# Two-layer graph network on one core: block turns behind the statistics, narrower edge-count columns, PSUM banks handed over singly

## Chip, cores and metric

One core of a Trainium2 chip. The metric is device microseconds of one execution, the median of several. PE is TensorE's matmul pipe, PEld its weight loads, DVE is VectorE, ACT ScalarE, POOL GpSimd, SP SyncE.

## Reference, cut to what matters

`N = 4096` nodes, 512 features, `adj` 4096 x 4096. Layer 0 is attention inside graphs of 128 nodes, layer 1 is graph attention over `adj`:

```python
h = relu(layernorm(x));  x = x + graph_attention(h, adj, ptr, Wq, Wk, Wv, ...)   # layer 0
h = relu(layernorm(x))
mx = einsum('nf,hfd->hnd', h, W)                                                 # layer 1, 8 heads of 64
attn = softmax(where(adj > 0, s_i + t_j, -inf))
x = x + einsum('hij,hjd->hid', attn, mx)
```

The factor from `s_i` cancels in the softmax, so the kernel forms e^t * mx and e^t for each node (520 numbers), multiplies them by the 0/1 mask, and divides.

## The kernel before

Layer 1 has two stages that matter here. Between the layers (about 360 to 460 us of the trace), each of 32 row tiles is normalised, transposed and projected (`project1`), then weighed by e^t on DVE (`weigh`) and split into a high and a low part. Tiles below 16 ("near") are transposed on PE. Tiles from 16 ("far") are turned on DVE in blocks of 32, written to DRAM and read back in the right layout. The far work runs eight tiles ahead of the projection. The order of DVE, ACT, POOL and SP is that of the source:

```python
for i in range(n, NT):
    far, near = i + AHEAD, i + 2
    if near + 1 < MIXED: load(near + 1)
    load(far + 2)
    if MIXED < far <= NT: turn(far - 1)              # DVE, waits for ACT's relu of that row
    if far % BY == 1 and MIXED + BY < far <= NT + 1: move(far // BY - 1)
    ...                                              # cut: first mask tile
    low()                                            # POOL: low part of tile i - 2
    if far < NT:     of[far] = moments(rows[far])    # DVE statistics, POOL rstd
    if near < MIXED: of[near] = moments(rows[near])
    if i + 1 < MIXED: relu_T(ps_t, rows[i + 1], hTs[i + 1])      # PE transposes, ACT relu
    pm = project1(ps_p, hTs[i], w1x)                 # PE, 8 matmuls
    if before: low = finish(*before, later=True)     # DVE weighing, ACT cast
    if near < MIXED: norm(rows[near], rows[near], of[near])
    if far < NT:     norm(rows[far], rows[far], of[far])
    e = weights(i, pm)                               # ACT exponential
    ...                                              # near tiles: four products on ACT
    if far < NT: nc.scalar.activation(rows[far], rows[far], AF.Relu)
```

Then the aggregation (about 460 to 950 us): for each row tile, 32 inner tiles times three column groups of 2 x 174 columns (high and low part of 174 numbers), accumulated in PSUM:

```python
D, H, EC, CB, CW1 = 512, 8, 520, 3, 174             # 3 * 174 = 522: two columns of ones count edges
def product(pg, at, part, j, c):
    nc.tensor.matmul(
        pg[:, : 2 * CW1], at[:, j, :], part(j)[:, c].rearrange("p s w -> p (s w)"),
        start=(j == 0), stop=(j == NT - 1),
    )
ps_g = straight.enter_context(tc.tile_pool(name="ps_g3", bufs=2, space=PSUM))
```

The edge count itself is used only in a general branch that these inputs do not take.

Of the kernel before, what the change touches and what calls it, by code (L numbers as in the profile page):

```python
# [23 lines left out]
NT = N // P  # L24
# [29 lines left out]
def kernel(  # L54
# [248 lines left out]
        widen(at, turn_words(sb, load_words(sb, i)))  # L303
        return at

    def product(pg, at, part, j, c):

        nc.tensor.matmul(  # L308
            pg[:, : 2 * CW1], at[:, j, :], part(j)[:, c].rearrange("p s w -> p (s w)"),
            start=(j == 0), stop=(j == NT - 1),  # L310
        )

    def aggregate(sb, ps_g, at, part):

        pg = ps_g.tile([P, CB, 512], F32, name="pg")
        for j in range(NT):
            for c in range(CB):
                product(pg[:, c], at, part, j, c)
        tot = sb.tile([P, EW], F32, name="tot")
        tot3 = tot.rearrange("p (c w) -> p c w", c=CB)  # L320
        nc.scalar.copy(tot3, pg[:, :, :CW1])  # L321
        nc.vector.tensor_tensor(tot3, tot3, pg[:, :, CW1 : 2 * CW1], ALU.add)  # L322
        return tot
# [48 lines left out]
    with ExitStack() as straight:  # L372
# [4 lines left out]
        with ExitStack() as prep:  # L377
# [262 lines left out]
            with tc.manual_schedule(engines={E.DVE, E.Activation, E.Pool, E.SP}):  # L640
                n = len(ahead) - 1
                hTs[n] = ahead[n]
                before = None
                for i in (1, 2):
                    load(n + i)
                for i in range(MIXED, n + AHEAD + 2):
                    load(i)
                norm(rows[n + 1], rows[n + 1])
                low = lambda: None
                for i in range(n, NT):  # L650
                    far, near = i + AHEAD, i + 2
                    if near + 1 < MIXED:
                        load(near + 1)
                    load(far + 2)
                    if MIXED < far <= NT:
                        turn(far - 1)
                    if far % BY == 1 and MIXED + BY < far <= NT + 1:
                        move(far // BY - 1)
                    if far == NT + 1:

                        begun.close()
                        sb3a = straight.enter_context(
                            tc.tile_pool(name="sb3a", bufs=1, side="right", reuse_waits="tile")
                        )
                        ata = sb3a.tile([P, NT, P], F32R, name="ata")
                        words = load_words(sb3a, 0)
                    if i == NT - 4:
                        at8 = turn_words(sb3a, words)
                    if i in (NT - 3, NT - 2):
                        half = (i - NT + 3) * NW // 2  # L670
                        widen(ata, at8, half, half + NW // 2)
                    low()
                    if far < NT:
                        of[far] = moments(rows[far])
                    if near < MIXED:
                        of[near] = moments(rows[near])
                    if i + 1 < MIXED:
                        hTs[i + 1] = sb2.tile([P, KC, P], F32, name="hT1")
                        relu_T(ps_t, rows[i + 1], hTs[i + 1])
                    pm = project1(ps_p, hTs[i], w1x)  # L680
                    if before:
                        low = finish(*before, later=True)
                    if near < MIXED:
                        norm(rows[near], rows[near], of[near])
                    if far < NT:
                        norm(rows[far], rows[far], of[far])
                    e = weights(i, pm)
                    halves = (1, 0)
                    if i < MIXED:
                        halves = (0,)  # L690
                        for h in range(H // 2, H):
                            nc.scalar.mul(
                                e[:, ts(h, HD)], pm[1][:, ts(h - H // 2, HD)],
                                e[:, ES + h : ES + h + 1],
                            )
                    before = (e, pm, part_tile(lo if i < LO else hi, i), halves)
                    if far < NT:
                        nc.scalar.activation(rows[far], rows[far], AF.Relu)  # L698
                low()
                finish(*before)  # L700
# [4 lines left out]
        sb3 = straight.enter_context(  # L705
            tc.tile_pool(name="sb3", bufs=2, side="right", reuse_waits="tile")
        )
        ps_g = straight.enter_context(tc.tile_pool(name="ps_g3", bufs=2, space=PSUM))
        nc.gpsimd.memset(held, 1.0)

        atb = sb3.tile([P, NT, P], F32R, name="atb", bufs=1)
# [46 lines left out]
        for c in (CB - 1, 0, 1):  # L758
            if c == 1:
                pg = ps_g.tile([P, CB, 512], F32, name="pg")[:, 0]  # L760
            else:
                pg = ps_l.tile([P, 512], F32, name="pl")
            for j in range(NT):
                product(pg, at, lambda j: parts[j], j, c)
            part = tot[:, ts(c, CW1)]
            nc.scalar.copy(part, pg[:, :CW1])
            nc.vector.tensor_tensor(part, part, pg[:, CW1 : 2 * CW1], ALU.add)
            if c == CB - 1:
                r = heads_rest(tot)
                nc.vector.tensor_scalar(held[:, 5:6], tot[:, ES : ES + 1], 0.0, None, ALU.is_gt)  # L770
                all_held = small.tile([P, 1], F32, name="all_held")
                nc.vector.tensor_reduce(all_held, held, AX.X, ALU.min)
                nc.vector.tensor_copy(
                    rb[:, :D].rearrange("p (h d) -> p h d", d=HD),
                    r[:, :, None].to_broadcast([P, H, HD]),
                )
            if c == 0:
                pt = ps_g.tile([P, CB, 512], F32, name="pg")[:, 0, :P]
                nc.tensor.transpose(pt[:1, :], all_held, ident)
                least = small.tile([1, 1], F32, name="least")  # L780
                nc.vector.tensor_reduce(least, pt[:1, :], AX.X, ALU.min)
                nc.vector.tensor_scalar(bad_i, least, 1.0, None, ALU.is_lt)
            here = slice(c * CW1, min((c + 1) * CW1, D))
            nc.vector.tensor_tensor(tot[:, here], tot[:, here], rb[:, here], ALU.mult)
            nc.vector.tensor_tensor(tot[:, here], tot[:, here], row[:, here], ALU.add)
            nc.scalar.dma_start(out[ts(i, P), here], tot[:, here])
# [3 lines left out]
    with tc.If(bad > 0, label="general"):  # L790
# [131 lines left out]
        with (  # L922
# [60 lines left out]
            with tc.For_i(0, n_levels, 1):  # L983
# [29 lines left out]
                with (  # L1013
                    tc.tile_pool(name="sb5", bufs=1) as sb,
                    tc.tile_pool(name="ps_g5", bufs=1, space=PSUM) as ps_g,
                    tc.For_i(0, NT, 1) as i,
                ):
                    sofar = sb.tile([P, D], F32, name="sofar")
                    nc.sync.dma_start(sofar, out[ds(i * P, P), :])
                    at = load_mask(sb, i, sb.tile([P, NT, P], F32R, name="at"))  # L1020
                    tot = aggregate(sb, ps_g, at, lambda j: parts_e[:, j])
                    alone = small.tile([P, 1], F32, name="alone")
                    nc.vector.tensor_scalar(alone, tot[:, EC : EC + 1], 0.0, None, ALU.is_equal)
                    n_alone = small.tile([P, 1], F32, name="n_alone")
                    nc.vector.tensor_scalar(n_alone, alone, float(N), None, ALU.mult)
                    den = small.tile([P, H], F32, name="den")
                    nc.vector.tensor_scalar(den, tot[:, ES:EC], n_alone, 1e-30, ALU.add, ALU.max)
                    num = tot[:, :D]
                    nc.vector.scalar_tensor_tensor(num, mx_sum, alone, num, ALU.mult, ALU.add)
                    row = done[:, ds(i, 1), :].rearrange("p o h -> p (o h)")  # L1030
                    take = small.tile([P, H], F32, name="take")
                    nc.vector.tensor_scalar(take, den, ACCEPT, None, ALU.is_ge)
                    nc.vector.tensor_tensor(take, take, row, ALU.is_gt)
                    nc.vector.tensor_add(row, row, take)
                    r = small.tile([P, H], F32, name="r")
                    nc.vector.reciprocal(r, den)
                    nc.vector.tensor_mul(r, r, take)
                    scaled(num, r)
                    nc.vector.tensor_add(num, num, sofar)
                    nc.sync.dma_start(out[ds(i * P, P), :], num)  # L1040
# [38 lines left out]
```

## Time and profile before

| | before |
|---|---|
| time, median | 959.8 us (first three runs), 959.05 us (five runs) |
| span in the trace | 956.0 us |
| PE busy | 934.7 us |
| last transposes of `row` to first aggregation matmul | 360.37 to 460.46 us, 100.09 us |
| first start to last end of the aggregation's matmuls | 460.46 to 950.37 us, 489.91 us |

The last two rows cut the trace at marks, so that drift of the first 360 us stays out. I call the first of them the passage. Its marks in PE's timeline of before (columns: start, length, engine, line, operation, tiles, shapes, count, and in brackets the idle time before and what ended it):

```profile
360.37 0.60 PE L136 MATMUL pt<-ident,row 128*128 128x128 f32 x4
460.46 15.53 PE L308 MATMUL pg<-part,ata 128*128 128x348 f32 x96 [0.61 <-DVE e L268]
```

Timeline of PEld in the kernel before:

```profile
408.52 3.37 PEld L259 LDWEIGHTS pp<-w1x,hT 128*128 128x128 f32 x16 [2.21 <-issue]
412.26 3.37 PEld L259 LDWEIGHTS pp<-w1x,hT 128*128 128x128 f32 x16 [0.37 <-issue]
415.96 3.37 PEld L259 LDWEIGHTS pp<-w1x,hT 128*128 128x128 f32 x16 [0.32 <-issue]
419.75 3.37 PEld L259 LDWEIGHTS pp<-w1x,hT 128*128 128x128 f32 x16 [0.41 <-issue]
```

The same time in the timeline of PE matmuls:

```profile
408.56 51.30 PE L259 MATMUL pp<-w1x,hT 128*128 128x264 f32 x224 [1.84 <-DVE e L268]
```

PE seems busy for 51.30 us without a break (this view joins records across idle times under 0.15 us; the busy time from 408.56 to the first aggregation matmul at 460.46 sums to 51.15 of 51.90 us). The loads show a break after every 16, that is after every tile, and tiles 3.74 us apart.

### The profile page before, as it was taken

Reading aid. Unit: us, or ns where it says so; the run is one execution under the profiler, and the core shown is the slowest. Engines: PE = TensorE matmul, PEld = TensorE weight load, DVE = VectorE, ACT = ScalarE, POOL = GpSimd, SP = SyncE. Lnnn points to the kernel's source line nnn. Section 1 sums busy time; section 2 is a strip of 40 time slices with the busy share of each in tenths; the row PEclk is TensorE's granted clock in tenths of the full one; section 3 lists DMA queues with packets and bytes.
Section 4 is the critical chain, followed back from the end, with each engine's and each line's share of the span. In section 5 each row is a group of like instructions: output and inputs, shape, how many; then the busy total and the mean of one; then the engine's idle time right before and its main releaser. Section 6 shows DMA issues by size and latency. Waiting matters only on the chain.

```text
span 956.0 us, 13142 instructions
## 1 busy us (share of the span) xinstructions
PE 934.7 (98%) x4987; PEld 810.8 (85%) x4987; DVE 465.0 (49%) x992; ACT 267.9 (28%) x539; POOL 179.9 (19%) x344
## 2 busy tenths in 40 slices
PE   8999999999999999999999999999999999999997
PEld 5676667776666777778999999999999999999997
DVE  4678877775775445674445242423324242423322
ACT  5776576666662224532000000000000000000000
POOL 2311213211211224655210100101010110101010
PEclk9999999999999999999999999999999999999999
DMA  9989889998985213575131312122231313222111
GB/s 343 417 344 390 332 312 364 348 367 322 367 349 199 78 34 110 165 198 133 56 85 49 88 50 84 51 82 72 61 89 45 89 50 83 57 77 85 48 45 36
DMA packets 61062, 156.63 MB, mean 164 GB/s; under 512 B 6722, under 2 KB 23490, under 8 KB 52290
## 3 DMA queue, kind: packets, MB, share of 16 engines
q1 hardware_dynamic: 51058, 138.70, 42.0%
q10 hardware_dynamic: 9936, 17.05, 4.8%
q8 instruction: 40, 0.66, 0.3%
q14 instruction: 28, 0.23, 0.1%
HBM read 117.97 MB, written 37.75 MB: 163 GB/s over the span
## 4 chain that ended last, share of the span: by engine, by line
PE 86%; DVE 4%; DMA 4%; ACT 3%; issue 1%; POOL 1%; SPq 0%; ACTq 0%; DVEq 0%
PE pg L308 50%; PE pp L457 12%; PE pp L445 10%; PE pp L259 5%; PE pp L530 3%; PE pss L503 3%; PE pt L136 1%; DMA row<-x_d 1%; DVE stats L118 1%; DMA a<-adj 1%; PE pl L308 1%; DVE blocks L623 1%; ACT rowm L698 1%; POOL rstd L124 1%; DMA mw<-a_d 1%
## 5 line engine op out<-in xcount | busy, mean ns | idle before, releaser
L308 PE MATMUL pg<-part,ata 128*128 128x348 f32 x1536 | 247.4, 322 | 0.6 <-DVE e L268 0.6
L308 PEld LDWEIGHTS pg<-part,ata 128*128 128x128 f32 x1536 | 245.0, 188 | 1.0 <-issue 1.0
L308 PE MATMUL pg<-part,atb 128*128 128x348 f32 x1472 | 237.3, 322 | 0.0
L308 PEld LDWEIGHTS pg<-part,atb 128*128 128x128 f32 x1472 | 235.0, 188 | 0.1
L321 ACT COPY tot<-pg 128x522 f32<-128x522 f32 x31 | 18.6, 599 | 455.9 <-PE pg L308 455.9
L480 ACT ACTIVATE junk<-a 128x2048 bf16<-128x2048 f32 (+15 forms) x92 | 124.5, 1353 | 49.9 <-DVE x L532 28.0
L259 PE MATMUL pp<-w1x,hT 128*128 128x256 f32 (+1 forms) x512 | 117.0, 384 | 2.0 <-DVE e L268 1.8
L457 PE MATMUL pp<-wv,hT 128*128 128x512 f32 x256 | 116.4, 598 | 0.0
L445 PE MATMUL pp<-hT,m_sb 128*128 128x256 f32 x512 | 113.2, 379 | 0.0
L259 PEld LDWEIGHTS pp<-w1x,hT 128*128 128x128 f32 x512 | 95.3, 190 | 19.3 <-issue 4.7
L296 DVE CAST atb<-at 128x4096 fp32r<-128x4096 fp8e4 x16 | 36.7, 2293 | 153.1 <-PE pg L308 153.1
L445 PEld LDWEIGHTS pp<-hT,m_sb 128*128 128x128 f32 x512 | 96.2, 190 | 12.8 <-issue 0.5
L296 DVE CAST ata<-at 128x4096 fp32r<-128x4096 fp8e4 (+1 forms) x17 | 37.3, 2196 | 141.8 <-PE pg L308 141.8
L457 PEld LDWEIGHTS pp<-wv,hT 128*128 128x128 f32 x256 | 49.2, 192 | 61.8 <-issue 61.8
L146 DVE TENSOR_SCALAR a<-a 128x512 fp8e4<-128x512 f32 x256 | 98.8, 466 | 1.6 <-DMA a_d<-a 1.4
L733 POOL COPY den_all<-tot 128x1 f32<-128x1 f32 x31 | 5.7, 184 | 367.9 <-DVE tot L322 355.9
L737 POOL TENSOR_TENSOR tot<-tot,row 128x512 f32<-128x512 f32 x31 | 39.9, 1286 | 61.9 <-DVE tot L327 57.8
L122 POOL TENSOR_SCALAR ve<-mv 128x1 f32<-128x1 f32 x64 | 16.3, 258 | 163.3 <-DVE mv L120 163.3
L243 POOL TENSOR_TENSOR part<-e,part 128x522 fp32r<-128x522 f32 x32 | 42.8, 1336 | 18.5 <-ACT part L240 18.4
L287 DVE STREAM_TRANSPOSE at<-mw 128x1024 f32<-128x1024 f32 x32 | 39.6, 1238 | 5.3 <-DMA mw<-a_d 5.3
L124 POOL TENSOR_TENSOR rstd<-ve,neghalf 128x1 f32<-128x1 f32 x64 | 38.5, 604 | 4.6
L461 DVE TENSOR_TENSOR v<-pp,bv_sb 128x512 f32<-128x512 f32 x32 | 22.0, 689 | 32.2 <-PE pp L457 32.2
(113 smaller groups left out, 691.0 us busy)
## 6 DMA issues: line engine op xcount, KB each, us to landing
a<-adj SPq DMA_DIRECT2D x64, 1024.0 KB, 12.8
a_d<-a SPq DMA_DIRECT2D x32, 512.0 KB, 10.1
mw<-a_d SPq DMA_DIRECT2D x128, 128.0 KB, 4.0
row<-x_d SPq DMA_DIRECT2D x41, 256.0 KB, 3.5
xg<-x SPq DMA_DIRECT2D x16, 512.0 KB, 4.6
x_d<-x ACTq DMA_DIRECT2D x32, 256.0 KB, 4.2
out<-tot ACTq DMA_DIRECT2D x31, 256.0 KB, 3.7
rowm<-x_d SPq DMA_DIRECT2D x16, 256.0 KB, 4.8
```

What stands on the lines that cost most here:

```text
L124: nc.gpsimd.tensor_tensor(rstd, ve, neghalf, ALU.pow)
L146: nc.vector.tensor_scalar(a8v[:, u], av[:, u], 0.0, None, ALU.is_gt, saturate=False)
L243: nc.gpsimd.tensor_sub(dst[:, :, 1, :], e3, dst[:, :, 0, :].bitcast(F32))
L259: nc.tensor.matmul(pm[g][:, :n], hT[:, k, :], w1x[:, k, g * HW : g * HW + n], start=(k == 0), stop=(k == KC - 1),)
L287: nc.vector.transpose(at8.rearrange("p c n b -> p (c n b)").bitcast(F32).rearrange("p (c u n) -> p c u n", c=NW, n=B), mw.rearrange("p u ( ...
L296: nc.vector.tensor_copy(at[:, c0 * BY : c1 * BY].rearrange("p (c b) q -> p c b q", b=BY), at8[:, c0:c1].rearrange("p c q b -> p c b q"),)
L308: nc.tensor.matmul(pg[:, : 2 * CW1], at[:, j, :], part(j)[:, c].rearrange("p s w -> p (s w)"), start=(j == 0), stop=(j == NT - 1),)
L445: nc.tensor.matmul(pp[:, : G * P], m_sb[:, k, ts(m, P)], hT[:, k, :], start=(k == 0), stop=(k == KC - 1),)
L457: nc.tensor.matmul(pp, hT[:, k, ts(t, P)], wv[:, k, :], start=(k == 0), stop=(k == KC - 1))
L480: nc.scalar.activation(junk[:, c0:c1], a[:, c0:c1], AF.Exp, scale=2.0 * NEG, accum_out=sums[:, n : n + 1],)
L503: nc.tensor.matmul(pss[:, t, :], gT[:, k, ts(t, P)], hT[:, k, ts(t, P)], start=(k == 0), stop=(k == KC - 1),)
L737: nc.gpsimd.tensor_add(num, num, row)
```

## The change

The intent: DVE need not wait for ACT's relu while statistics of another, loaded row could be taken; the columns of ones need no matmul except one that defines the PSUM cells; and the first aggregation tile needs only three banks, which were free long before.

```diff
-    def product(pg, at, part, j, c):
+    def product(pg, at, part, j, c, count):
+        n = CW1 if count or j == 0 else min(CW1, EC - c * CW1)
         nc.tensor.matmul(
-            pg[:, : 2 * CW1], at[:, j, :], part(j)[:, c].rearrange("p s w -> p (s w)"),
+            pg[:, : 2 * CW1].rearrange("p (s w) -> p s w", s=2)[:, :, :n],
+            at[:, j, :], part(j)[:, c, :, :n],
             start=(j == 0), stop=(j == NT - 1),
         )
...
                     load(far + 2)
-                    if MIXED < far <= NT:
-                        turn(far - 1)
...
                     if near < MIXED:
                         of[near] = moments(rows[near])
+                    if MIXED < far <= NT:
+                        turn(far - 1)
...
-        ps_g = straight.enter_context(tc.tile_pool(name="ps_g3", bufs=2, space=PSUM))
+        ps_g = straight.enter_context(
+            tc.tile_pool(name="ps_g3", bufs=2, space=PSUM, reuse_waits="tile")
+        )
```

(The callers pass `count`, true only in the general branch. "One row tile" means the inner tile j = 0.)

More of the change, by code (lines that the diff above doesn't have):

```diff
@@ L304, in load_mask, with aggregate @@
         return at
-    def product(pg, at, part, j, c):
+    def product(pg, at, part, j, c, count):
+        n = CW1 if count or j == 0 else min(CW1, EC - c * CW1)
         nc.tensor.matmul(
-            pg[:, : 2 * CW1], at[:, j, :], part(j)[:, c].rearrange("p s w -> p (s w)"),
+            pg[:, : 2 * CW1].rearrange("p (s w) -> p s w", s=2)[:, :, :n],
+            at[:, j, :], part(j)[:, c, :, :n],
             start=(j == 0), stop=(j == NT - 1),
         )
-    def aggregate(sb, ps_g, at, part):
+    def aggregate(sb, ps_g, at, part, count=False):
         pg = ps_g.tile([P, CB, 512], F32, name="pg")
@@ L317, in aggregate @@
             for c in range(CB):
-                product(pg[:, c], at, part, j, c)
+                product(pg[:, c], at, part, j, c, count)
         tot = sb.tile([P, EW], F32, name="tot")
@@ L763 @@
             for j in range(NT):
-                product(pg, at, lambda j: parts[j], j, c)
+                product(pg, at, lambda j: parts[j], j, c, False)
             part = tot[:, ts(c, CW1)]
@@ L1020 @@
                     at = load_mask(sb, i, sb.tile([P, NT, P], F32R, name="at"))
-                    tot = aggregate(sb, ps_g, at, lambda j: parts_e[:, j])
+                    tot = aggregate(sb, ps_g, at, lambda j: parts_e[:, j], count=True)
                     alone = small.tile([P, 1], F32, name="alone")
```

## The prediction

> **What bounds the kernel now.** I read the page first, then the waits of TensorE (PE), the chain of waits, and busy time by stretch. The page's chain by engine says who sets the end:
>
> ```profile
> PE 86%; DVE 4%; DMA 4%; ACT 3%; issue 1%; POOL 1%; SPq 0%; ACTq 0%; DVEq 0%
> ```
>
> PE is busy for 934.7 us of a 956.0 us span, so a change can gain only by giving PE less to do or by closing its gaps. The three parts of the change touch 340 to 480 us, the passage between the layers, and the aggregation (462 to 950 us). PE's waits in 340 to 480:
>
> ```profile
> PE pp L259 <- DVE e L268: 1.8, 1, 1.8
> PE pt L136 <- DVE rown L130: 1.8, 3, 0.9
> PE pg L308 <- DVE e L268: 0.6, 1, 0.6
> ```
>
> Busy time in stretches of 2 us over the same window sums to 135.47 of 140 us, an idle time of 4.53 us. I place it as 0.88 in 376 to 380, 0.44 in 380 to 392, 0.44 in 392 to 396, 1.90 in 404 to 410 (together 3.66), 0.10 at 448 and 0.61 at the handover at 460; the rest is crumbs. That is the whole prize of the two scheduling parts. The chain shows why VectorE (DVE) is late. One turn of the loop that still transposes rows for PE:
>
> ```profile
> 378.81 0.59 ACT rowm L698
> 379.42 0.71 DVE blocks L623
> 380.13 0.59 DVE stats L118
> 380.74 0.18 DVE mv L120
> 380.92 0.59 DVE stats L118
> 381.54 0.18 DVE mv L120
> 381.72 0.32 DVE e L268
> ...
> 382.67 0.18 ACT e L401
> 382.87 0.93 ACT e L692 x4
> 383.81 0.64 ACT rowm L698
> ```
>
> The reader is to see a closed ring: relu on ScalarE (ACT), block turn, two sets of statistics, weighing, exponential, four products, relu again, 5.00 us a turn (383.81 less 378.81). PE needs 3.95 us for such a tile (3.51 for 16 records of L259 and 0.44 for four transposes in the chain, 365.33 to 369.28). So PE is held in this phase. A turn of the later loop, without near rows:
>
> ```profile
> 413.42 0.64 ACT rowm L698
> 414.08 0.71 DVE blocks L623
> 414.79 0.59 DVE stats L118
> 415.40 0.19 DVE mv L120
> ...
> 415.97 0.57 POOL rstd L124
> 416.57 0.56 DVE rowm L130
> 417.15 0.64 ACT rowm L698
> ```
>
> It takes 3.73 us, against 3.63 us of PE work (the timeline has 155 records in 35.15 us, 16 to a tile). Nearly balanced, so the lag from the first loop is never worked off.
>
> Last, the aggregation: the forms of matmul, and L308 alone in 50 us:
>
> ```profile
> L308 PE MATMUL pg<-part,ata 128*128 128x348 f32 x1536 | 247.4, 322 | 0.6 <-DVE e L268 0.6
> L457 PE MATMUL pp<-wv,hT 128*128 128x512 f32 x256 | 116.4, 598 | 0.0
> L445 PE MATMUL pp<-hT,m_sb 128*128 128x256 f32 x512 | 113.2, 379 | 0.0
> 500.00:550.00 50.00, 50.00 (x316) 50.00 (x315) 1.00 0.27 76
> ```
>
> 316 matmuls in 50 us is 158 ns each at full clock and without a gap; the 322 ns in the group is a latency with overlap, and multiplying by it would double any saving.
>
> **What the Trainium skill says.** "TensorE: Matmul & The Clock Gate", section "Back-to-back issue gap", gives a warm gap of N/2.4 + 2.5 ns and adds that in a stream of weight loads and matmuls both set the spacing. For N = 348 that is 147.5 ns; the trace has 158, so the constant is larger here, but what I need is the slope. The trace supports it: 256 more columns cost 598 - 379 = 219 ns, and those f32 matmuls show two records each, so if I take two passes to a record it is 0.43 ns per column and pass, next to 1/2.4 = 0.417. "PSUM — Partial Sum Buffer", section "Engine vs sequencer instructions", says VectorE's queue is strict FIFO: a turn that waits for ACT holds the statistics behind it, though their row is loaded. The ring above agrees (stats follow the turn at once). "SBUF — State Buffer", section "Door 1: The DMA port swizzle", warns that a non-contiguous PSUM access pattern "significantly slows down matmuls". No matmul of the kernel before has such an output in this stage, so its trace cannot say.
>
> **Part 1, the turn behind the statistics.** Nothing is added or removed; the order view shows the turn after the statistics and ahead of weighing, in every tile. The wait for relu now lies beside the statistics. The near ring loses 381.72 - 380.13 = 1.59 us: 5.00 - 1.59 = 3.41 us, under PE's 3.95. In the later loop, statistics (0.82) run beside relu (0.64), and the rstd work of POOL (0.23 + 0.57 and gaps) beside turn (0.71) and weighing (0.72): the DVE ring becomes 0.82 + 0.71 + 0.72 + 0.56 = 2.8 us, under 3.63. I looked for a second ring, through POOL: count copy 0.4, low part 1.5, two rstd pairs 1.7, two norms 1.0, relu 0.6, turn 0.7, weighing 0.4, cast and exponential 0.8, that is 7.1 us over two tiles or 3.6 a tile; tight against 3.95, but under. The order view also shows that PE's transposes now stand wholly ahead of each projection, where the kernel before split some projections around them. So both loops should be PE's again and the 3.66 us should go, with the 0.10. I count 3.4 us: a first tile or two may still wait.
>
> **Part 2, the edge count for one row tile.** Two columns of 522 hold ones for counting edges, in two halves. Group c = 2 now has 2 x 172 = 344 columns instead of 348, for 31 of 32 inner tiles, in each of 32 row tiles: 992 matmuls. At 4 x 0.417 = 1.67 ns this is 1.65 us, all of it on PE and so on the path. Against it stands that operand and result become two runs with a gap of 8 bytes each. The weights are loaded as before.
>
> **Part 3, banks singly.** The first aggregation waited for the last weighing (0.61 us), because the new pool took over all old banks at once. The order view has its first matmul wait for DVE and ACT before, and for Pool alone after. The first tile takes the banks of the old transposes, long read; the banks of the last projection come later, and the last part is needed only by the 94th matmul, some 15 us on. I count 0.6 us.
>
> Sum: 3.4 + 1.65 + 0.6 = 5.65 us. 959.8 - 5.65 = 954.15, so **954.1 us**.
>
> **Rivals.** First: the split pattern slows the matmul. If a gap cost 5 ns, 992 x 5 = 5.0 us would cancel nearly all, 959 us; at 20 ns it is 19.8 us, 974 us. For it is the skill's warning; against it, only one jump per matmul, on an even column (174), and a stage where PE already has 13 ns beyond 348/2.4. I give a visible penalty one chance in eight. Second: the ring through POOL or a DMA wait takes the place of the one removed. For it are the 5.27 us that DVE waits at 447 for the mask words, behind the last block write; but that write follows the last turn, which comes sooner, and PE lost just 0.10 us there. If half the gaps stayed, 956 us. Third: only the column cut works and the gaps merely move (PE waits for hT from DRAM instead), 958 us. The hT loads stand ahead of their use by several us, so I think little of it. Fourth: the c = 2 matmul gets no faster, since weight load or a fixed step sets the 158 ns; PEld is busy through this stage. Then 955.8 us.
>
> **Range and chances.** The first three numbers of before lie within 1.1 us, so the noise is about half a us each way. Everything working in full is 3.76 + 1.65 + 0.61 = 6.0 us, 953.8; a bit of slack below that for the aggregation gaining by its better ends gives a low end of 951.5. Half the gaps staying and no column gain gives 957.5 as the high end. Faster by over 2% would need 19 us, three times all that the parts can reach: 0.01. Slower by 2% needs 25 ns of penalty on each split matmul (24.8 us over 992): 0.02. Within 2%: 0.97.
>
> **What would show it.** Part 1 right: between 370 and 460 us no wait of pt for rown and none of pp for e above 0.2 us in sum, statistics ahead of turn on DVE, and the first L308 matmul some 3.5 to 4.3 us earlier than 460.46. Part 3 right: no gap between the last L259 and the first L308 matmul. Part 2 right: some 317 instead of 316 matmuls in 50 us (a mean spacing of 158.2 - 1.67/3 = 157.7 ns), so the aggregation is 1.65 us shorter from first matmul to last. Wrong: a longer latency or spacing of the 2 x 172 form than of 348, or PE gaps of the same size now released by POOL, ACT or DMA.

## The result, and the profile after

The changed kernel took **948.61 us** (median of 5 runs, 947.67 to 950.48), against 959.05 us (957.88 to 959.97) for the kernel before. Ratio 0.9893, 95% interval 0.9878 to 0.9907. The direction was right and the change is under 2%, as forecast, but the time lies below the predicted range: 10.4 us were gained by the medians, where I had 5.65.

| | before | after | gain | predicted |
|---|---|---|---|---|
| span in the trace | 956.0 | 946.8 | 9.2 | 5.65 |
| passage, 360.60 to 452.91 us after | 100.09 | 92.31 | 7.78 | 4.0 |
| aggregation, 452.91 to 941.27 us after | 489.91 | 488.36 | 1.55 | 1.65 |

So the aggregation gave what it should, and the whole surplus is in the passage. PE's waits between 340 and 480 us are now one line, in place of the three that the prediction shows:

```profile
PE pp L259 <- DVE e L268: 0.2, 1, 0.2
```

And the timelines of PE and of PEld, first PE with the passage's start and its second half:

```profile
360.60 0.60 PE L136 MATMUL pt<-ident,row 128*128 128x128 f32 x4
...
389.52 35.23 PE L259 MATMUL pp<-w1x,hT 128*128 128x264 f32 x160
424.97 28.29 PE L259 MATMUL pp<-w1x,hT 128*128 128x264 f32 x128 [0.22 <-DVE e L268]
452.91 15.60 PE L310 MATMUL pg<-part,ata 128*128 128x348 f32 x96
```

then PEld:

```profile
389.41 34.94 PEld L259 LDWEIGHTS pp<-w1x,hT 128*128 128x128 f32 x160
424.94 27.92 PEld L259 LDWEIGHTS pp<-w1x,hT 128*128 128x128 f32 x128 [0.59 <-issue]
```

Here the loads show one break instead of one per tile. 128 records take 27.94 us from start to the next group's start (452.91 - 424.97), 0.2183 us each, so 16 of them, a tile, need 3.49 us. Now the 224 records of before can be judged: they need 224 x 0.2183 = 48.9 us, but 51.90 us passed from 408.56 to the first aggregation matmul. Of these 3.0 us of loss PE's idle view shows 0.61 and the sum of its busy time 0.75. A matmul's recorded length is about 380 ns at a step of 218, so it reaches some 160 ns past the next one's due start and covers that much of every break. The first half hides less of its loss: from the passage's start to the 224 records PE took 48.19 us before (360.37 to 408.56) and 42.94 for the same matmuls after, 5.25 us lost, of which busy time showed 3.72 (44.47 busy).

DVE's timeline in the near loop after the change has the statistics ahead of the turn, and the turn starts without an idle time:

```profile
376.11 0.69 DVE L118 BATCH_NORM_STATS2 stats<-rowm 128x6 f32<-128x512 f32 x1
376.83 0.18 DVE L120 BATCH_NORM_AGGREGATE mv<-stats 128x2 f32<-128x6 f32 x1
376.93 0.66 DVE L118 BATCH_NORM_STATS2 stats<-rown 128x6 f32<-128x512 f32 x1
377.62 0.18 DVE L120 BATCH_NORM_AGGREGATE mv<-stats 128x2 f32<-128x6 f32 x1
377.72 0.68 DVE L626 STREAM_TRANSPOSE blocks<-rowm 128x512 f32<-128x512 f32 x1
```

### The profile page after: what moved, and what is told of

Same layout as the page of the kernel before. It is cut to its first block, busy times and chain, and to the rows that moved or that the text cites. A ratio compares the mean times of both kernels' runs of the same rounds, so it can differ in the third digit from the quotient of the medians.

```text
span 946.8 us, 13144 instructions
## 1 busy us (share of the span) xinstructions
PE 929.3 (98%) x4987; PEld 809.7 (86%) x4987; DVE 464.3 (49%) x992; ACT 268.7 (28%) x539; POOL 176.9 (19%) x344
## 4 chain that ended last, share of the span: by engine, by line
PE 90%; DMA 4%; DVE 2%; ACT 2%; issue 1%; POOL 1%; SPq 0%; ACTq 0%
PE pg L310 50%; PE pp L259 11%; PE pp L460 11%; PE pp L448 9%; PE pp L533 3%; PE pss L506 3%; DMA a<-adj 2%; PE pt L136 2%; DMA row<-x_d 1%; PE pl L310 1%; DVE a L146 1%; ACT junk L483 1%; DMA bv_sb<-bv 1%; ACT gT L452 0%; POOL rstd L124 0%
## 5 line engine op out<-in xcount | busy, mean ns | idle before, releaser
L310 PE MATMUL pg<-part,ata 128*128 128x348 f32 (+1 forms) x1536 | 246.7, 321 | 0.0
L259 PE MATMUL pp<-w1x,hT 128*128 128x256 f32 (+1 forms) x512 | 114.9, 383 | 0.2 <-DVE e L268 0.2
L460 PEld LDWEIGHTS pp<-wv,hT 128*128 128x128 f32 x256 | 48.9, 191 | 61.6 <-issue 61.6
L243 POOL TENSOR_TENSOR part<-e,part 128x522 fp32r<-128x522 f32 x32 | 41.2, 1287 | 17.3 <-ACT part L240 17.2
```

The source lines that it names most:

```text
L243: nc.gpsimd.tensor_sub(dst[:, :, 1, :], e3, dst[:, :, 0, :].bitcast(F32))
L259: nc.tensor.matmul(pm[g][:, :n], hT[:, k, :], w1x[:, k, g * HW : g * HW + n], start=(k == 0), stop=(k == KC - 1),)
L310: nc.tensor.matmul(pg[:, : 2 * CW1].rearrange("p (s w) -> p s w", s=2)[:, :, :n], at[:, j, :], part(j)[:, c, :, :n], start=(j == 0), stop= ...
L460: nc.tensor.matmul(pp, hT[:, k, ts(t, P)], wv[:, k, :], start=(k == 0), stop=(k == KC - 1))
```

## The experiments

Theory R: the DVE ring set PE's pace in both loops, and PE's idle view showed only half of the loss. Rivals: the surplus comes from the bank handover (H); from PE's order, which the scheduler changed as a side effect (O): with the turn moved, PE's transposes stand ahead of each projection, where three projections of before are split around them (not the seven that I wrote for e4); or the ring theory holds only for the 3.7 us that I had seen. Each run's profile gives the passage:

| run | passage, us | ratio to before (95%) |
|---|---|---|
| before / after | 100.09 / 92.31 | 0.9893 (0.9878 to 0.9907) |
| e1 turn only | 93.24 | 0.9932 (0.9915 to 0.9950) |
| e2 columns only | 100.06 | 0.9988 (0.9968 to 1.0007) |
| e3 banks only | 99.19 | 0.9998 (0.9979 to 1.0018) |
| e4 PE order only | 100.19 | 1.0011 (0.9995 to 1.0027) |
| e5 turn, near loop only | 94.59 | 0.9931 (0.9915 to 0.9948) |
| e6 / e12 turn, later loop only | 101.38 / 97.97 | 0.9954 (0.9934 to 0.9974) / one look |
| e11 e6 with other loads | 97.44 | 0.9979 (0.9957 to 1.0002) |
| e7 after + one statistic | 92.17 | 0.9892 (0.9867 to 0.9916) |
| e8 after + two statistics | 95.44 | 0.9941 (0.9924 to 0.9958) |
| e10 after with other loads | 92.31 | 0.9908 (0.9886 to 0.9930) |
| e9 passage as in after, result wrong | 93.19 | not comparable |

Times of single runs scatter by up to 6 us (before: 954.64 to 958.65 in one batch, where the runs at a granted TensorE clock of 0.999 or 1.0 of full speed have spans of 952.9 to 954.3 us and those at 0.996 to 0.998 have 954.8 to 956.9), so for effects of 1 us the passage decides, not the ratio. But each passage is read from one profile. Pairs with the same code in the passage: 100.09 and 100.06 (before, e2), 92.31 and 93.19 (after, e9), 101.38 and 97.97 (e6, e12). In the last two pairs a wait for `hT`, the part of the later rows that comes back from DRAM, makes the difference, so a difference of 1 us counts only where the gap that changed is seen.

### e1, e2, e3: each part alone

e1 is the kernel before with only the moved turn of the diff, e2 with only `product`, e3 with only `reuse_waits="tile"`.

> The kernel before with the turn moved behind the statistics and nothing else. In the trace of before the aggregation's first matmul starts at 460.46 us, in that of the changed kernel at 452.91. Theory R (the VectorE ring held TensorE in both loops, and TensorE's idle view hid about half of the loss, because the modelled ends of matmuls cover gaps of up to 0.4 us): first aggregation matmul at about 453.6, that is 6.9 us sooner than before, with the 0.6 us gap at the handover still there; time ratio about 0.993 (-7 us). Rival as I predicted (only the visible 3.7 us): 456.8 and ratio 0.996. Rival H (most of the extra gain comes from the handing over of banks): 457 or later.

> Only the narrower matmuls of the last column group. First to last aggregation matmul took 489.9 us before and 488.4 in the changed kernel. If the 1.55 us come from four columns fewer in 992 matmuls: 488.4 us here as well, ratio 0.998 to 0.999, first aggregation matmul at 460.4 as before. If the split pattern cost anything that another part made up for, the stretch is over 489 us.

> Only the banks handed over singly. Theory R: the gap of 0.6 us before the first aggregation matmul goes, which starts 0.6 to 0.8 us sooner (459.7 to 459.9), ratio 0.999 to 1.000. Rival H: 2 us or more sooner, since the handover then freed more than the visible gap.

e1: 950.45 us (956.59 before), passage 100.09 - 93.24 = **6.85 us** shorter, as theory R says; the gap at the handover is still there:

```profile
454.11 11.07 PE L308 MATMUL pg<-part,ata 128*128 128x348 f32 x68 [0.61 <-DVE e L268]
```

e2: 955.88 us, a ratio that alone shows nothing (the interval holds 1), but the aggregation in its trace runs from 459.94 to 948.18, 488.24 us, **1.67 us** less than before, and the passage is unchanged. e3: 957.05 us, passage **0.90 us** shorter (from the mark at 408.5 us to the aggregation 51.02 instead of 51.90 us, so the gain is at the handover), a little over the expected 0.6 to 0.8, and far from rival H's 2 us. The visible gap was 0.61, the gap of the weight loads 0.98. The parts add up: 6.85 + 0.90 = 7.75 of 7.78 us in the passage, and 1.67 beside 1.55 in the aggregation. So most of the surplus is in the turn: 6.85 us for 3.4 predicted.

### e4: PE's order alone

```diff
-            with tc.manual_schedule(engines={E.DVE, E.Activation, E.Pool, E.SP}):
+            with tc.manual_schedule(engines={E.PE, E.DVE, E.Activation, E.Pool, E.SP}):
```

> The kernel before, turn in its old place, but TensorE's order taken from the source: transposes ahead of each projection, the same order as with the turn moved (seven projections of before are otherwise split around transposes). Rival O (the changed order of TensorE, a side effect, made the extra gain): first aggregation matmul 3 us or more sooner than 460.46. Theory R: the ring is as long as before, so no gain: 460 to 462 us, ratio 1.000 to 1.002, with longer gaps ahead of the transposes in place of the split ones.

958.33 us, ratio 1.0011, passage 100.19 us. PE's order is now that of e1, and nothing is gained, so rival O falls as a cause of its own (whether the order adds anything once the turn is moved, no run separates). The run also holds the clearest picture of what PE's row hides. First PE, then PEld:

```profile
410.14 51.41 PE L259 MATMUL pp<-w1x,hT 128*128 128x264 f32 x224 [0.38 <-DVE e L268]
```

```profile
413.86 3.37 PEld L259 LDWEIGHTS pp<-w1x,hT 128*128 128x128 f32 x16 [0.37 <-issue]
417.55 3.37 PEld L259 LDWEIGHTS pp<-w1x,hT 128*128 128x128 f32 x16 [0.33 <-issue]
```

51.41 us of "busy" for 48.9 us of work.

### e5, e6, e12: the turn moved in one loop only

e5 moves the turn while `near < MIXED` and leaves it ahead otherwise; e6 is the reverse:

```diff
-                    if MIXED < far <= NT:
+                    if MIXED < far <= NT and near >= MIXED:     # e6: near < MIXED
                         turn(far - 1)
...
+                    if MIXED < far <= NT and near < MIXED:      # e6: near >= MIXED
+                        turn(far - 1)
```

> The kernel before, the turn behind the statistics only while near rows are still being normalised; in the later loop it stays ahead. Measure: from the last transposes of row at 360.4 us to the first aggregation matmul, 100.1 us before, 93.2 with the whole turn moved. Theory R: the later ring is still longer than TensorE's work (3.73 against 3.51 us a tile, over some ten tiles, 2.2 us in all), but VectorE no longer starts it late, and TensorE may run two tiles ahead, so the lag stays inside that lead: 93.2 to 94.5 us. If instead each ring takes its own share of the gain: 93.2 plus the later loop's loss, about 96 us or more.

> The other half: the turn moved only in the later loop; TensorE's order is the same as in the kernel before. Theory R: the near loop loses what it lost before (five turns of 5.05 us, 2.9 us in all), the later ring becomes shorter than TensorE's 3.51 us and works the lag off, so no gaps after the first two or three later tiles: 96 to 97 us from the last transposes of row to the first aggregation matmul, weight-load gaps of 0.3 to 0.4 us per tile after 410 us gone. The two halves then save more together (about 6.5 and 3.5 us) than the 6.9 of both. A rival that gives the gain to TensorE's changed order says 100 us.

> The same kernel as e6_far_only, for a second profile. There TensorE waited 4.0 us at two places for rows coming back turned from DRAM (weight-load gaps of 1.93 and 2.30 us), and 101.4 us passed from the last transposes of row to the first aggregation matmul, though the median of its four runs was 4 us below the kernel before. If those waits were a matter of that one execution: no such gap here and 96 to 98 us. If the DMA round trip is the next bound of this arrangement: a gap of 1.5 us or more again.

e5: 951.76 us (958.34 before), passage 94.59 us, just above the expected band of 93.2 to 94.5. The near loop alone brings 5.50 of the 6.85 us. The later loop, left as it was, then costs only 1.35 us more than in e1: started without lag, it spends the lead that PE's buffers give first, and the breaks come back only after 406 us.

e6 was a miss in its profile: 101.38 us, *longer* than before, though its four runs (952.55 to 958.02) have a median of 954.31. In the profiled execution, which was the slowest of the four, PE waited twice for rows that were turned, written to DRAM and read back, 1.93 and 2.30 us by the weight loads. The second look, e12, has 97.97 us, inside the band, and one of the two waits again, here in PE's waits and on PEld:

```profile
PE pp L259 <- DMA hT<-hT_d: 1.5, 1, 1.5
```

```profile
415.18 13.89 PEld L259 LDWEIGHTS pp<-w1x,hT 128*128 128x128 f32 x64 [1.91 <-issue]
429.68 27.92 PEld L259 LDWEIGHTS pp<-w1x,hT 128*128 128x128 f32 x128 [0.60 <-issue]
```

So both readings held in part. The breaks per tile are gone after the loop, as theory R says: 64 and 128 loads run through, where before each tile had its break. And the round trip through DRAM is the next bound: the wait comes back as a wait for `hT`. The first of the two waits (tile 20) was there in both looks, because the blocks were turned late: their write to DRAM was issued 41.7 us into the passage in both, 37.3 us in the changed kernel, and landed after 4.4 us in all three. At the second (tile 24) it was the landing that differed: the write took 6.47 us in e6 and 4.44 in e12, and PEld's gap was 2.30 and 0.60 us. Why a write lands late in some executions stays open. It does not need a late near loop: in e9 below, whose passage has the code of the changed kernel, that write took 6.17 us (4.43 in the changed kernel), and PE waited 1.10 us:

```profile
PE pp L259 <- DMA hT<-hT_d: 1.1, 1, 1.1
```

With e12 the later loop alone brings 2.1 us, with e6 it loses 1.3; the ratio of e6's four runs stands for 2.5 to 6.3 us of gain. I had expected the halves to save more together (some 6.5 and 3.5) than both at once; whether they overlap as far as that is not settled by such scatter.

### e11, e10: other loads

The later rows are loaded by ACT's queue, in e11 on e6, in e10 on the changed kernel:

```diff
-                    nc.sync.dma_start(rows[i], x1_d[i])
+                    (nc.scalar if i > MIXED + 3 else nc.sync).dma_start(rows[i], x1_d[i])
```

> e6_far_only with the loads of later rows issued by ScalarE's queue in place of SyncE's, where they stood behind the moves that wait for a block to land in DRAM (VectorE waited 3.5 us for such a row at 411 us in e6_far_only). If that wait passes on to TensorE: it goes, and 96 to 98 us pass from the last transposes of row to the first aggregation matmul. If the round trip of the blocks themselves is too long: TensorE waits for hT as before, 99 us or more.

> A try at a better version: the changed kernel with the later rows loaded by ScalarE's queue. In the changed kernel VectorE waited 2.35 us for a row at 408.7 us and TensorE lost 0.22 us at 425. Expected: the VectorE wait under 0.5 us, TensorE's 0.22 us gone, 92.1 instead of 92.3 us, and no change that the time can show (ratio to the kernel before 0.989, as the changed kernel).

e11: 954.92 us, passage 97.44 us; DVE's wait for a row fell from 3.48 to 0.40 us, yet PEld's gap at 412 us stayed, 1.83 us. The two were not cause and effect, and the gap belongs to the late blocks: their write was issued 41.7 us into the passage and landed after 4.45 us, as in e6 and e12 (the waits view names DVE's norm as releaser here, so this reading is not confirmed by it). What did go is the smaller gap at tile 24, 0.60 us in e12. e10: 948.43 us (957.62 before), passage 92.31 us, exactly that of the changed kernel. Of DVE's waits of 1.66 and 2.35 us for rows one of 0.63 us is left, and PE keeps its 0.2 us (at 411 instead of 425 us). So the try at a better version gained nothing: those DVE waits lay inside the lead. No version here beats the changed kernel.

### e7, e8: lengthening the ring on purpose

```diff
                     if MIXED < far <= NT:
                         turn(far - 1)
+                    if near >= MIXED and far < NT:
+                        for _ in range(1):                          # e8: range(2)
+                            extra = small.tile([P, 6], F32, name="extra")
+                            nc.vector.bn_stats(extra, rows[far])
```

> The changed kernel with one more statistics instruction (0.69 us) after the turn in the later loop, its result unused. The trace of the changed kernel shows turns 2.7 to 3.2 us apart where nothing else held VectorE. Theory R: 3.4 to 3.9 us against TensorE's 3.51, inside the two-tile lead: 92.3 to 93.3 us from the last transposes of row to the first aggregation matmul (92.3 without it).

> Two more of them. Theory R: the ring becomes 4.1 to 4.6 us, VectorE falls 0.6 to 1.1 us behind on each of some ten tiles, 6 to 11 us, of which the lead takes 3.5 to 7: 93.5 to 98 us, with weight-load gaps back in the later loop. If the ring did not set TensorE's pace, 92.3 us as without them.

e7: 948.2 us and 92.17 us, no cost, a shade below the band. e8: 952.78 us (958.34 before) and 95.44 us, 3.1 us longer than the changed kernel, and the break per tile is back on PEld:

```profile
409.85 3.37 PEld L259 LDWEIGHTS pp<-w1x,hT 128*128 128x128 f32 x16 [0.53 <-issue]
413.76 3.37 PEld L259 LDWEIGHTS pp<-w1x,hT 128*128 128x128 f32 x16 [0.54 <-issue]
```

In that time DVE works without idle time, turns starting 3.96 us apart (407.53 to 411.49), and PE's tiles 3.91 us apart. DVE's turn of the loop, not PE's work, is the clock here, and the changed kernel has room for one more such instruction but not for two.

### e9: slope of a matmul's columns

```diff
-        n = CW1 if count or j == 0 else min(CW1, EC - c * CW1)
+        n = CW1 if count or j == 0 else (CW1, CW1 - 24, EC - 2 * CW1)[c]
```

> Wrong on purpose: the changed kernel with 2 x 150 instead of 2 x 174 columns in the middle column group for 31 of 32 inner tiles, 48 columns fewer in 992 matmuls. If a column costs 1/2.4 = 0.417 ns and a split run nothing: 19.8 us off the 488.4 us from first to last aggregation matmul, 468.5 us. If the step of 158 ns is set by the weight load or another fixed time, or if two short runs cost something: 472 us or more, up to 488.

931.8 us (958.67 before; result wrong, relative error 0.07), aggregation from 453.87 to 924.89, 471.02 us: 17.3 us less than the changed kernel, not 19.8. That is 17.5 ns per matmul, or 0.364 ns per column. In the last row tile, where each column group runs alone, the 32 matmuls of the middle group step by 139.7 instead of 160.6 ns from start to start (the first step, 244 ns in both, left out), which is 20.8 ns for the 48 columns, the full slope. Why 2.5 ns per matmul are missing where three groups alternate (the larger jump in the pattern, or the weight loads) stays open. For the four columns of the change it does not show: 1.67 us over 992 matmuls is 1.68 ns each, against 1.67 by the slope.

## Why the prediction was wrong

**Mechanism of part 1: right.** Moving the turn took the statistics out of the ring, PE's waits for `rown` went, of those for `e` 0.2 us is left, and in the changed kernel's profile no other wait took their place (e1, e4, e8; for e9 see the rivals). The estimate of the later ring was good too: 2.8 us; where nothing held DVE, turns stand 2.73 us apart in the changed kernel (417.61 to 420.34).

**Its size: the step that failed** is "Busy time in stretches of 2 us over the same window sums to 135.47 of 140 us, an idle time of 4.53 us" with "That is the whole prize of the two scheduling parts." Idle time of PE is not the loss, because the recorded ends of matmuls cover short breaks: in before the passage lost 5.25 us in its first half and 3.0 in its second, where busy time showed 3.72 and 0.75. The term of 3.4 us measured 6.85 us (e1), part 3's 0.6 measured 0.90 (e3). The page "Perfetto Trace Analysis" of the Trainium skill gives the ground for this, in its section "Tensor Engine Instruction (MATMUL, LD_WEIGHTS)": the end of a TensorE record is estimated, "a model, not a measurement"; and in "Identifying the Most-Contended Engine" it sends the reader to the weight loads' busy share. This trace agrees: a row of 51.30 us shown as busy for 48.9 us of work.

**The same slip in another place:** "It takes 3.73 us, against 3.63 us of PE work (the timeline has 155 records in 35.15 us, 16 to a tile)." Those 35.15 us were already the held pace. PE's need is 3.49 us (after), and my own chain showed 3.51 for 16 records a paragraph earlier. The two numbers disagreed and I used the wrong one; "nearly balanced" was a loss of 0.2 us on each of several tiles. A smaller misreading: "316 matmuls in 50 us is 158 ns each" counts matmuls that only reach into the window; from start to start they step by 159.4 ns. And 147.5 ns is, by the section that the prediction cites, the gap of an isolated matmul, not of a stream. Neither entered the sum, which used the slope alone.

**Part 2: right**, 1.65 us predicted, 1.67 measured alone (e2). The rival of a slowed split pattern did not occur, and neither did the one of a step that columns do not set (e9).

**Part 3: right** in mechanism, the last bit again being hidden time.

**Rivals.** The third ("PE waits for hT from DRAM instead") was thought little of, and did not happen in the profile of the change, but it did in e6 and e12, and in e9, where the same passage code waited 1.10 us for `hT` and took 0.88 us longer. So the loads do not stand far enough ahead of their use in every execution. The low end, 951.5, came from the idle sum plus a little; it inherited the error. Corrected, the sum is 6.85 + 1.67 + 0.90 = 9.4 us, in line with the 9.2 us between the traces and inside the interval of the measured ratio (8.9 to 11.7 us of 959.05).

## What to carry to other kernels

To see what PE loses, compare steps, not busy time: start to start of equal groups of matmuls, in a held and in an unheld stretch, or read the gaps of the weight loads; breaks shorter than the recorded reach of a matmul past its successor's start, here some 160 ns, do not show as idle. Where one engine's loop is a ring through others, ask which independent work can be placed between the sender and the waiter; here that freed 6.9 us without removing one instruction. And mend the stage that comes first: the near loop alone brought 5.5 us, since the later one could then live on the lead, while the later loop alone showed 2.1 us of gain in one profile and a loss of 1.3 in the other (e5 against e12 and e6).

## What the Trainium skill lacked or had wrong

- "TensorE: Matmul & The Clock Gate", section "Back-to-back issue gap": N/2.4 + 2.5 ns gives 147.5 ns at N = 348, for an isolated matmul; for a stream of loads and matmuls the section measures about 131 ns at N = 512, and says nothing of this shape and type. Here, in such a stream, the step from start to start was 159.4 ns with three column groups alternating, above both. The formula's slope held: 1.68 ns for 4 columns, 20.8 ns for 48 in the lone group, but 17.5 ns for 48 where the groups alternate.
- "SBUF — State Buffer", section "Door 1: The DMA port swizzle": a non-contiguous PSUM pattern "significantly slows down matmuls". Two runs of 172 columns with a jump of two fp32 cost nothing that could be measured (1.67 us saved of 1.65 expected, over 992 matmuls). Whether the jump of 24 columns cost the 2.5 ns of e9 is open.
- "Perfetto Trace Analysis" has the rule that I missed, but no figure for how much PE's busy time can hide: here about 0.2 us per break, 2.2 of the 3.0 us lost in the passage's second half and 1.5 of 5.25 us in its first.
